# One transfer for the maxima of four heads, and the fills of the spare rows moved to the projections, in a decoder layer

## The chip, the cores and the metric

The kernel runs on one core of a Trainium2 chip. The metric is the device time of one execution in microseconds (us). The kernel before has a median of 663.38 us over three runs (662.83 to 667.53).

## The reference

A pre-norm decoder layer on x of shape (4, 1024, 256), in float32. What matters here are the two attentions, with 16 heads of 16 features each:

```python
# S: windowed causal attention, windows of W = 128 rows, each row sees its window and the one before
scores = jnp.einsum('bhcqd,bhckd->bhcqk', qc, kcat) / HD ** 0.5
scores = jnp.where(mask[None, None], scores, -jnp.inf)
attn = jax.nn.softmax(scores, axis=-1)
out = jnp.einsum('bhcqk,bhckd->bhcqd', attn, vcat)
...
# X: attention on a context of 77 rows
scores = jnp.einsum('bhqd,bhkd->bhqk', q, k) * scale
scores = jnp.where(mask == 0, jnp.asarray(-jnp.inf, scores.dtype), scores)
attn = jax.nn.softmax(scores, axis=-1)
...
x = x + attn_S(layernorm(x)); x = x + attn_X(layernorm(x), ctx); x = x + ffn(layernorm(x))
```

The feed-forward part quantises its inputs and weights to 8 bits; it is not touched by the change.

## The kernel before, in words

Attention is done in eight jobs, one for each batch and kind, in the order S0, S1, S2, X0, S3, X1, X2, X3. A job has two groups g of eight heads. q and k lie transposed, features on partitions: a group's tile has four slots of SL = 32 partitions, and a slot holds two heads of 16 features. Of each tile there are two copies, o = 0 and o = 1. In the products for head o, one operand has the other head's 16 rows masked to zero, so that a matmul over 32 rows gives the scores of one head. The rows of the other head are therefore spare, and one of them, row (1 - o) * 16 of each slot, carries the maxima: q holds the negated maximum of each query row there, k holds ones, and so the second product comes out with the maximum already taken off.

The steps of a group (g, o), by function:

- `project` (L346): 16 matmuls (L306) into ps_p, then on ScalarE two passes: L377 copies ps_p into one copy of q or k, L378 makes the masked other copy. For X jobs (q alone) L364 and L367 do this, and two transfers (L371) fill spare rows of the odd copy with zeros and ones.
- `maxima` (L724): the scores with queries on partitions, 16 records of L735 for each unit of two row tiles (S) or 32 of L750 (X), read by VectorE (L765 with the causal mask, L776) into mx. An S group has four units, an X group two.
- `put_maxima` (L784): a transpose of mx (L787), a copy to mxT of 32 x 128 on ScalarE (L791), for S jobs a transfer that fills the ones row of k (L793), and four transfers (L801), one for each slot, that write mxT's rows into the spare row of q.
- `weights` (L816): the scores with keys on partitions (L827 for S, L856 for X), which read the put rows, then the exponential on ScalarE (L837, L859) and for S the causal mask on POOL (L841).
- `weighted_values` (L862): L871 and L881, then VectorE transposes (L895) and normalises.

The order is written out by a small planner at the end of `attention`: a list of units, and in slot s the weights of unit s and the maxima of unit s + 5 (LEAD). Projections, values, output projections and preparations of weights are put into slots by due times and costs; within a slot come weighted values, these tasks, then `put_maxima`, `maxima`, `weights`. Each engine gets its instructions in that order and runs them in it. `put_maxima` of a group stands one slot before its first weights for S jobs, three for X jobs.

All these transfers go out on SP's queue (queue_of[0]), in the order written: rows of maxima, fills, and the loads of weights still to come (the context weights L471, the context L491, the feed-forward weights L629 and L656). An instruction on SP waits for its inputs and holds up those behind it. The first halves of the first job are projected before a branch on the mask (L1555); the branch taken here is the one with equal mask rows.

Of the kernel before, what the change touches and what calls it, by code (L numbers as in the profile page):

```python
# [13 lines left out]
AF = mybir.ActivationFunctionType  # L14
# [4 lines left out]
P = 128  # L19
# [6 lines left out]
def decoder_layer(  # L26
# [32 lines left out]
    nc = tc.nc  # L59
    B, S, D = x.shape  # L60
    SK = ctx_in.shape[1]
    FF = w_gate.shape[0]
    NT = S // P
    NC = D // P
    H, HD, SL = 16, 16, 32
    NP = 2
    NS = 2
    NJ = 4
    NH = 2
    HT = NT // NH  # L70
# [131 lines left out]
    with ExitStack() as att:  # L202
# [7 lines left out]
        def bank(name):  # L210
            return ps_b.tile([P, 512], F32, name=name, tag="b")
# [5 lines left out]
        rows, onerow, nextrow = [], [], []  # L217
        for o in range(NS):
# [3 lines left out]
            for dst, first, n in (  # L222
# [7 lines left out]
                    out=at[:, :, 0:n],  # L230
                    in_=at[:, :, 0:n],
                    compare_op=ALU.not_equal,
                    fill=1.0,
# [10 lines left out]
        none_one = []  # L244
        for row in range(2):
            t = wp.tile([NJ, P], F32, name=f"fill{row}")
# [5 lines left out]
            out=f,  # L252
            in_=f,
            compare_op=ALU.is_ge,
            fill=NEG,
# [20 lines left out]
        def next_of(key, tiles):  # L276
            turn[key] += 1
            return tiles[(turn[key] - 1) % len(tiles)]
# [24 lines left out]
        def by_columns(out, lhsT, rhs, **on):  # L303
            for k in range(NJ):
                r = slice(k * SL, (k + 1) * SL)
                nc.tensor.matmul(out[r], lhsT[:, r], rhs, skip_group_check=True, **on)  # L306
# [24 lines left out]
        def normed_T(job, hf):  # L331
# [11 lines left out]
                    nc.scalar.copy(xnT[:, c, :], ps)  # L343
            job.xnT[hf] = xnT

        def project(job, g, which, hf):  # L346

            out = job.q if which == "q" else job.k
            w = job.wq if job.kind == "X" else (wq_s if which == "q" else wk_s)
            if hf == 0:  # L350
                for o in range(NS):
                    out[g, o] = next_of("qk", qks)
            ps = bank("ps_p")
            for c in range(NC):
                by_columns(
                    ps,
                    w[:, c, g * P : (g + 1) * P],
                    job.xnT[hf][:, c, :],
                    start=(c == 0),
                    stop=(c == NC - 1),  # L360
                )
            half = [out[g, o][:, hf * HS : (hf + 1) * HS] for o in range(NS)]
            if job.kind == "X":
                nc.scalar.activation(  # L364
                    half[1], ps, AF.Identity, bias=job.bq[:, g : g + 1], scale=QSCALE
                )
                nc.scalar.activation(  # L367
                    half[0], half[1], AF.Identity, bias=nextrow[0], scale=rows[0]
                )
                for row in range(2):  # L370
                    queue_of[0].dma_start(  # L371
                        out=half[1][row : P : SL, :].rearrange("j (t q) -> j t q", q=P),
                        in_=none_one[row].unsqueeze(1).to_broadcast([NJ, HT, P]),
                    )
                return
            first = 1 if which == "q" else 0
            nc.scalar.activation(half[first], ps, AF.Copy, scale=QSCALE if which == "q" else 1.0)  # L377
            nc.scalar.activation(half[1 - first], half[first], AF.Copy, scale=rows[1 - first])  # L378


        leading = Job("S", 0)
        for hf in range(NH):
            st = stats_of(leading, hf)
            st.tiles(0, HT, True)
            st.end()
            normed(leading, hf, range(HT))
            if hf == 0:
                masked = wgT.rearrange("p c f -> p (c f)")[:, : NT * SK]
                nc.vector.tensor_scalar(masked, m_all, 0.0, None, ALU.is_equal)
                ones_bf = wuT[:, 0, 0:P]  # L390
                nc.gpsimd.memset(ones_bf, 1.0)
                normed_T(leading, 0)
                for which in ("q", "k"):
                    project(leading, 0, which, 0)
                ps_n = bank("ps_n")
                for t in range(NT):
                    nc.tensor.matmul(
                        ps_n[:, :SK],
                        ones_bf,
                        masked[:, t * SK : (t + 1) * SK],  # L400
                        start=(t == 0),
                        stop=(t == NT - 1),
                    )
# [12 lines left out]

        begun = dict(turn)
        begin.close()
        queue_of = [nc.sync]

        def attention(alike):
            turn.update(begun)
            queue_of[0] = nc.sync if alike else nc.scalar
# [6 lines left out]
            for i in range(5):  # L430
                t = wp.tile([P, 2, H + 1, HD + 1], F32, name=f"vt{i}")
# [352 lines left out]
            def put_maxima(job, g, o):  # L784

                ps = bank("ps_mx")
                nc.tensor.transpose(  # L787
                    ps[: NJ * NT, :P], job.mx[g, o].rearrange("p j t -> p (j t)"), ident
                )
                mxT = work.tile([NJ * NT, P], F32, name="mxT", tag="mxT", bufs=2)  # L790
                nc.scalar.copy(mxT, ps[: NJ * NT, :P])  # L791
                if job.kind == "S":
                    queue_of[0].dma_start(  # L793
                        out=job.k[g, o][(1 - o) * HD : P : SL, :].rearrange(
                            "j (t q) -> j t q", q=P
                        ),
                        in_=none_one[1].unsqueeze(1).to_broadcast([NJ, NT, P]),
                    )
                for j in range(NJ):
                    row = j * SL + (1 - o) * HD  # L800
                    queue_of[0].dma_start(  # L801
                        out=job.q[g, o][row : row + 1, :],
                        in_=mxT[j * NT : (j + 1) * NT, :],
                    )

            def weight_bias(job, g, o, u):

# [304 lines left out]
            first, last = -LEAD, N + 8  # L1112
# [23 lines left out]
            def project_all(job, g, hf, *when):  # L1136
                for which, (a, by) in zip(("q", "k") if job.kind == "S" else ("q",), when):
                    task(a, by, 1.0, project, job, g, which, hf)

            for j, job in enumerate(jobs):  # L1140
# [4 lines left out]
                for hf in range(NH):  # L1145
# [41 lines left out]
                    g = NP - 1  # L1187
# [43 lines left out]
            for slot in range(first, last):  # L1231
# [6 lines left out]
                if slot == N:  # L1238
# [7 lines left out]
                    while beside:  # L1246
                        t = min(beside, key=lambda t: t[1:3])
# [13 lines left out]
                while t := next_in(tasks, slot, spent, cap):  # L1261
# [3 lines left out]
                    if fn is out_project:  # L1265
                        job, hf, t2 = args
# [9 lines left out]
                for args in puts.get(slot, ()):  # L1276
                    put_maxima(*args)
# [332 lines left out]
```

## Time and profile before

| | |
|---|---|
| median of three runs | 663.38 us (662.83 to 667.53) |
| profiled execution, its own time | 661.71 us |
| its span | 660.0 us |
| mean granted TensorE clock | 0.986 |
| transfers of maxima (L801), 4 KB each | 128 |
| fills of X kind (L371), 8 KB each | 32 |
| ones fills (L793), 16 KB each | 16 |
| attention, S and X jobs | about 18 to 540 us |

How to read the lines: "PE" is TensorE's matmuls, "PEld" its weight loads, "DVE" VectorE, "ACT" ScalarE, "POOL" GpSimd, "SPq" the queue on which transfers are issued. A line of the timeline gives start, length, engine, source line, operation, output and inputs, number of instructions merged, and in brackets how long the engine had been idle before and what ended that. A line of the view of one tile gives the number of instructions with their shortest, median and longest duration in ns, or an engine that waited for the tile with the time in us and how often. A line of the view by stretches gives busy us of each engine with the number of instructions in brackets, then the granted TensorE clock as a share of full speed, the busy share of the DMA engines and the GB/s moved.

### The profile page before, as it was taken

To read this page: it belongs to the slowest core of one execution; us is meant where nothing else is said; L and a number is where in the kernel's file an instruction comes from. 1 tells how busy PE (TensorE), PEld (TensorE's weight loads), DVE (VectorE), ACT (ScalarE), POOL (GpSimd) and SP (SyncE) were. 2 spreads that over 40 slices of the span, in tenths; PEclk is the share of its full clock that TensorE was granted. 3 is DMA by queue.
4 is the path that set the end of the run, shared out by engine and by line. 5 is a ranking of instruction groups with operands and counts; after the bars stand their busy time and mean duration, and the time that the engine had idled before them with its cause. 6 is when DMAs were issued, how large, how long until landed. Compare 5 with 4: busy or idle time off the path is not lost.

```text
span 660.0 us, 20192 instructions
## 1 busy us (share of the span) xinstructions
PE 607.4 (92%) x7862; PEld 347.5 (53%) x7862; DVE 541.5 (82%) x1915; ACT 366.8 (56%) x672; POOL 268.6 (41%) x522
## 2 busy tenths in 40 slices
PE   9899999999999989989999999999999997878774
PEld 6456556566565655544456655544434345334564
DVE  5778878788689798578997986888878787799896
ACT  2365655644656536455565365447466565698392
POOL 3164633645227487440064866526601141111032
PEclk9999999999999999799999999999999999899898
DMA  8100100000000000000000000000000110000057
GB/s 289 51 5 16 38 4 20 4 5 23 3 28 12 11 12 14 5 22 18 5 11 11 13 26 28 5 4 6 4 4 6 35 65 17 1 0 1 1 96 164
DMA packets 19293, 17.93 MB, mean 27 GB/s; under 512 B 3190, under 2 KB 18551, under 8 KB 19191
## 3 DMA queue, kind: packets, MB, share of 16 engines
q1 hardware_dynamic: 16999, 14.74, 7.0%
q0 software_dynamic: 1904, 1.84, 2.1%
q8 instruction: 64, 1.05, 0.6%
q14 instruction: 38, 0.31, 0.1%
q10 hardware_dynamic: 288, 0.00, 0.0%
HBM read 9.47 MB, written 6.03 MB: 23 GB/s over the span
## 4 chain that ended last, share of the span: by engine, by line
PE 56%; DVE 30%; ACT 6%; issue 6%; POOL 1%; DMA 1%; DVEq 0%; ACTq 0%
PE ps_p L306 11%; PE ps_av L871 7%; PE sc_n L735 7%; PE sc_t L827 6%; PE ps_op L306 6%; DVE junk L765 5%; PE ps_av L881 3%; DVE o_sb L895 3%; PE ps_v L306 3%; DVE bnst L192 2%; PE sc_n L750 2%; PE sc_t L856 2%; DVE aT L917 2%; PE ps_idle L117 2%; DVE x L935 2%
## 5 line engine op out<-in xcount | busy, mean ns | idle before, releaser
L765 DVE CUSTOM_DVE_ANT_0 junk<-sc_n,cboth 128x256 bf16<-128x256 f32 (+1 forms) x512 | 172.7, 403 | 33.1 <-PE sc_n L735 32.7
L837 ACT ACTIVATE pt<-sc_t 128x512 f32<-128x512 f32 (+1 forms) x256 | 125.4, 577 | 84.3 <-PE sc_t L827 83.1
L841 POOL TENSOR_SCALAR_AFFINE_SELECT pt<-pt 128x256 f32<-128x256 f32 x256 | 101.7, 407 | 113.1 <-ACT pt L837 102.9
L859 ACT ACTIVATE ptx<-sc_t 77x512 f32<-77x512 f32 x128 | 65.2, 596 | 36.1 <-PE sc_t L856 36.1
L827 PE MATMUL sc_t<-shared 32*128 32x256 f32 (+1 forms) x1024 | 79.8, 371 | 2.9 <-DMA shared<-mxT 1.8
L735 PE MATMUL sc_n<-shared 32*128 32x256 f32 (+1 forms) x1024 | 75.1, 387 | 2.7 <-ACT shared L377 1.2
L322 POOL TENSOR_SCALAR xn<-x,mv,rs 128x256 f32<-128x256 f32 x56 | 69.7, 1251 | 0.0
L827 PEld LDWEIGHTS sc_t<-shared 32*128 32x128 f32 x1024 | 61.6, 186 | 11.0 <-ACT mxT L791 2.7
L160 POOL TENSOR_SCALAR ve<-mv 128x4 f32<-128x4 f32 x20 | 4.6, 232 | 153.3 <-DVE mv L194 153.3
L895 DVE STREAM_TRANSPOSE o_sb<-ps_av 128x512 f32<-128x512 f32 x63 | 45.0, 714 | 24.4 <-PE ps_av L871 15.3
L306 PE MATMUL ps_p<-shared,w_s 128*32 128x512 f32 x512 | 60.9, 595 | 3.3 <-DVE mx L776 1.7
L735 PEld LDWEIGHTS sc_n<-shared 32*128 32x128 f32 x1024 | 46.1, 184 | 33.3 <-DVE mx L765 12.6
L871 PE MATMUL ps_av<-pt,vt 128*32 128x256 f32 (+1 forms) x1152 | 60.3, 353 | 3.0 <-DVE mx L765 2.6
L776 DVE TENSOR_REDUCE mx<-sc_n 128x4 f32<-128x308 f32 x128 | 51.8, 467 | 8.7 <-PE sc_n L750 8.5
L871 PEld LDWEIGHTS ps_av<-pt,vt 128*32 128x32 f32 x1152 | 35.5, 112 | 31.9 <-issue 6.9
L765 DVE DVE_READ_ACCUMULATOR2_ANT mx<- 128x1 f32 x512 | 42.9, 84 | 0.0
L856 PE MATMUL sc_t<-shared,kx 32*77 32x512 f32 x256 | 42.8, 598 | 0.0
L377 ACT ACTIVATE shared<-ps_p 128x512 f32<-128x512 f32 x32 | 19.1, 597 | 38.7 <-PE ps_p L306 38.7
L881 PE MATMUL ps_av<-ptx,vx 77*32 77x512 f32 x256 | 36.0, 605 | 4.8 <-DVE mx L776 3.1
L750 PEld LDWEIGHTS sc_n<-kx,shared 32*128 32x128 f32 x1024 | 31.7, 186 | 10.2 <-DVE mv L194 1.7
L750 PE MATMUL sc_n<-kx,shared 32*128 32x77 f32 x1024 | 36.4, 277 | 0.0
L1423 ACT ACTIVATE act<-pg,gsc 128x512 f32<-128x512 f32 x44 | 29.2, 687 | 11.6 <-PE pg L1408 8.9
(200 smaller groups left out, 990.7 us busy)
## 6 DMA issues: line engine op xcount, KB each, us to landing
x<-in_x_dram SPq DMA_DIRECT2D x8, 512.0 KB
out_dram<-shared SPq DMA_DIRECT2D x9, 256.0 KB
shared<-mxT SPq DMA_DIRECT2D x128, 4.0 KB
out_dram<-x SPq DMA_DIRECT2D x7, 256.0 KB
out_dram<-shared POOLq DMA_DIRECT2D x7, 256.0 KB, 4.5
w_s<-in_L_attn_w_qkv_dram SPq DMA_DIRECT2D x2, 384.0 KB
raw_d<-in_L_ffn_w_down_dram SPq DMA_DIRECT2D x2, 352.0 KB
raw_f<-in_L_ffn_w_gate_dram SPq DMA_DIRECT2D x5, 128.0 KB
```

What stands on the lines that cost most here:

```text
L306: nc.tensor.matmul(out[r], lhsT[:, r], rhs, skip_group_check=True, **on)
L322: eng.tensor_scalar(xn, xb[job.b][:, t, :], job.st[hf].mv[:, i, 0:1], job.st[hf].rs[:, i : i + 1], ALU.subtract, ALU.mult,)
L735: nc.tensor.matmul(banks[j][:, (i + 1) * 2 * P - n : (i + 1) * 2 * P], q[r, t * P : (t + 1) * P], k[r, k0 * P : k0 * P + n], start=True, s ...
L750: nc.tensor.matmul(banks[j][:, i * SK : (i + 1) * SK], q[r, t * P : (t + 1) * P], k[r, :], start=alike, stop=alike or i == HT - 1,)
L765: nc.vector.tensor_tensor_reduce(out=junk[:, 2 * P - n :], in0=banks[j][:, (i + 1) * 2 * P - n : (i + 1) * 2 * P], in1=cboth[:, 2 * P - n ...
L827: nc.tensor.matmul(banks[j][:, w : w + n], k[r, t * P : (t + 1) * P], q[r, t * P : t * P + n], start=True, stop=True,)
L837: nc.scalar.activation(pt.rearrange("p i a q -> p (i a q)")[:, :w], banks[j][:, :w], AF.Exp)
L841: nc.gpsimd.affine_select(out=pt[:, :, 0, :], in_=pt[:, :, 0, :], compare_op=ALU.is_ge, fill=0.0, base=0, pattern=[[0, 2], [1, P]], channe ...
L856: nc.tensor.matmul(banks[j][:SK], k[r, :], q[r, s], start=alike, stop=True)
L859: nc.scalar.activation(pt, banks[j][:SK], AF.Exp)
L871: nc.tensor.matmul(ps[j * SL : (j + 1) * SL, (a0 - t0) * P : (a1 - t0) * P], slot_of(job.vs[kb // 2][:, kb % 2], heads[j]), job.pts[g, o, ...
L895: nc.vector.transpose(job.av[g, o, hf], ps)
```

## The change

The four row transfers of `put_maxima` become one transfer with the 32 rows of mxT as its source and the spare row of all four slots as its target. The ones fill of k leaves `put_maxima`. In its place `project` fills spare rows beside every S projection: for q, the max row of the odd copy is set to zero over the half that was projected; for k, the ones row of the even copy is filled by a transfer, and the odd copy gets its ones from the bias of the second ScalarE pass (`onerow`, a 1 at that row), which was a plain scaled copy. The fills read `none_one`, two small tiles of zeros and ones; `queue_of` is made before the first projections. For X jobs the same two fills are issued as before, through the helper.

```diff
+        queue_of = [nc.sync]
+
+        def fill(half, row, value):
+            queue_of[0].dma_start(
+                out=half[row : P : SL, :].rearrange("j (t q) -> j t q", q=P),
+                in_=none_one[value].unsqueeze(1).to_broadcast([NJ, HT, P]),
+            )
+
         def project(job, g, which, hf):
...
-                for row in range(2):
-                    queue_of[0].dma_start(
-                        out=half[1][row : P : SL, :].rearrange("j (t q) -> j t q", q=P),
-                        in_=none_one[row].unsqueeze(1).to_broadcast([NJ, HT, P]),
-                    )
+                fill(half[1], 0, 0)
+                fill(half[1], 1, 1)
                 return
             first = 1 if which == "q" else 0
             nc.scalar.activation(half[first], ps, AF.Copy, scale=QSCALE if which == "q" else 1.0)
-            nc.scalar.activation(half[1 - first], half[first], AF.Copy, scale=rows[1 - first])
+            if which == "q":
+                nc.scalar.activation(half[0], half[1], AF.Copy, scale=rows[0])
+                fill(half[1], 0, 0)
+            else:
+                nc.scalar.activation(
+                    half[1], half[0], AF.Identity, bias=onerow[1], scale=rows[1]
+                )
+                fill(half[0], HD, 1)
...
                 nc.scalar.copy(mxT, ps[: NJ * NT, :P])
-                if job.kind == "S":
-                    queue_of[0].dma_start(
-                        out=job.k[g, o][(1 - o) * HD : P : SL, :].rearrange(
-                            "j (t q) -> j t q", q=P
-                        ),
-                        in_=none_one[1].unsqueeze(1).to_broadcast([NJ, NT, P]),
-                    )
-                for j in range(NJ):
-                    row = j * SL + (1 - o) * HD
-                    queue_of[0].dma_start(
-                        out=job.q[g, o][row : row + 1, :],
-                        in_=mxT[j * NT : (j + 1) * NT, :],
-                    )
+                queue_of[0].dma_start(
+                    out=job.q[g, o][(1 - o) * HD : P : SL, :].rearrange(
+                        "j (t q) -> j t q", q=P
+                    ),
+                    in_=mxT,
+                )
```

`half` is the projected half of the tile's columns (HT = 4 tiles of 128), NJ is 4 slots, NT is 8 tiles.

More of the change, by code (lines that the diff above doesn't have):

```diff
@@ L418, in decoder_layer @@
         begin.close()
-        queue_of = [nc.sync]
         def attention(alike):
```

## The prediction

> **What bounds the kernel now.** I read the page first: busy times, then the slices and the granted clock.
>
> ```profile
> span 660.0 us, 20192 instructions
> PE 607.4 (92%) x7862; PEld 347.5 (53%) x7862; DVE 541.5 (82%) x1915; ACT 366.8 (56%) x672; POOL 268.6 (41%) x522
> ...
> PEclk9999999999999999799999999999999999899898
> ```
>
> TensorE is busy 92% of the span and VectorE 82%; the two pass scores and maxima to each other in a fixed order, so time is lost only where TensorE stands still and VectorE has no backlog to live on. The one 7 in the clock row (slice 17, about 264 to 280 us) is such a place. Next I asked who waits for the transfers that the change merges: the view of tile mxT.
>
> ```profile
> L801 SPq DMA_DIRECT2D shared<-mxT x128: 621/635/857, 32.2 to 525.0; - x128
> ...
> who waited for it (us, times):
>   PEld sc_t L827: 2.7, 6
>   PEld sc_t L856: 2.3, 4
>   PE sc_t L827: 2.1, 4
> ```
>
> One issue holds the SP queue 0.635 us, so the four of a group go out over 2.7 us; yet all waits for them come to a few us in 32 groups. The trace records every increment of a transfer's semaphore. By the last one, a row of maxima (L801) lands 1.78 us after its issue begins, a fill of the X kind (L371, 4 x 4 pieces of 512 B) 1.88, and a ones fill (L793, 4 x 8 pieces) 2.33. I set the last landing of each group against its first weight matmul (L827 or L856). All 16 X groups have 3.4 to 15 us to spare; of the S groups two are late by 0.96 and 1.80 us, both last of their batch, before an X job (265.46 and 396.01 us); four are late by 0.6 or less. The worst:
>
> ```profile
> 261.38 0.39 SPq L629 DMA_DIRECT2D raw_f<-in_L_ffn_w_gate_dram  x1
> ...
> 261.87 0.56 SPq L793 DMA_DIRECT2D shared<-fill  x1
> ...
> 262.52 2.75 SPq L801 DMA_DIRECT2D shared<-mxT  x4
> ...
> 265.46 3.14 PE L827 MATMUL sc_t<-shared 32*128 32x256 f32 x16 [1.30 <-DMA shared<-mxT]
> ...
> 268.52 3.64 PE L871 MATMUL ps_av<-pt,vt 128*32 128x128 f32 x40
> ```
>
> mxT was written at 260.27, but the queue held two X fills, a weight load and the ones fill first. The clock by stretches shows what the stall cost further:
>
> ```profile
> core 0: us, PE busy (x) PEld busy (x) DVE busy (x) ACT busy (x) POOL busy (x), PEclk, DMA share, GB/s
> ...
> 263.20:266.50 3.30, 2.00 (x38) 1.50 (x38) 1.63 (x4) 1.46 (x2) 0.76 (x2) 1.00 0.04 12
> 266.60:269.90 3.30, 3.30 (x30) 2.01 (x34) 0.00 (x0) 2.03 (x4) 1.20 (x3) 0.50 0.02 5
> 270.00:273.30 3.30, 3.30 (x34) 2.00 (x24) 1.00 (x3) 0.00 (x0) 1.10 (x2) 0.50 0.02 5
> ```
>
> After the gap TensorE ran 6.8 us at half clock, with VectorE idle for 6.43 us.
>
> **The change, part by part.** Counts on SP in the S and X jobs: 128 row transfers become 32, 16 ones fills go, 32 new fills come (one per q or k projection of an S job): 80 issues fewer. The merged put has the ones fill's outer shape (4 x 8 pieces), so I price its landing like L793, 2.33 us, with 1.78 (a row) as the low end. Before, the last row landed 2.06 + 1.78 = 3.84 us after the first issue; it is 1.5 us earlier now, and the weights wait once, not four times.
>
> Gains. (1) The group at 265.46: without the ones fill the put goes out at about 261.7 and lands at 264.05; TensorE is free at 264.1. Sc_t takes 1.04 us (its length in groups that do not wait), the ps_av after it 1.94 (the same work at 398.98), ps_t 1.06 (at 16.86): ps_mx, at 273.63 before, can start at about 268.2. Gain 5.4; if the clock drops all the same, 2. The xn tiles are there early (POOL ends them at 260.8), so nothing else is late next. (2) The group at 396.01: it ended at 399.05; the put now leaves at 393.1, right behind the 352 KB raw_d load, which landed at 395.62 (the ones fill behind it at 395.70), so 395.9 + 1.04 = 396.9: gain 2.1, between 1.0 and 2.5. (3) The four small ones are 0.77, 0.41, 0.26 and 0.33 longer than 1.04; after the first TensorE waits for VectorE anyway (37.23 us). I take 0.5 of 1.77. Sum: 8.0.
>
> Losses: the new waits. A maxima matmul (L735) now waits for a fill after the projection's second ScalarE pass, on q for odd heads and on k for even ones. q fills have at least 15 us to their reader. k fills need about 2.0 us (0.09 because the pass with bias is 0.813 as in L367 and not 0.722 as in L378, 0.03 to issue, 1.88); 13 of 16 have 4.1 us or more. Three have none:
>
> ```profile
> 16.86 1.06 PE L337 MATMUL ps_t<-ident,xn 128*128 128x128 f32 x8
> 18.64 1.80 PE L735 MATMUL sc_n<-shared 32*128 32x128 f32 x32 [0.72 <-ACT shared L343]
> 20.39 3.64 PE L306 MATMUL ps_p<-shared,w_s 128*32 128x512 f32 x32
> 24.77 2.01 PE L735 MATMUL sc_n<-shared 32*128 32x256 f32 x32 [0.74 <-ACT shared L377]
> ```
>
> (4) The first maxima, 18.64: the k pass ends at 18.04 (L378), so by the row the fill lands at 20.03; but the last two x loads, ahead on the same queue, land at 19.44 and 20.69, and a small transfer behind a big one landed 0.08 after it (395.70). I take 20.7: +2.1, between 1.4 and 2.7. (5) Maxima of tile 4, 24.77: pass ends 25.47, landing 27.47: +2.7. (6) The same in batch 3, TensorE at 315.28: pass ends 315.98, landing 317.98; VectorE had other work until 316.71 and would get its scores 1.16 later (as 25.93 after 24.77), at 319.1: +2.4. What queues behind these waits is all of TensorE's stream, and VectorE with it.
>
> SP order: fills that wait for ScalarE now stand ahead of weight loads. With the ScalarE ends of the trace, craw leaves 9.1 us later (lands 84.5, read at 90.5: free), Wv 8.0 later (landing 123.7 against a read at 122.59: (7) +1.1), Wq 9.8 later (173.7 against 173.39: (8) +0.3), one raw_f 11.8 later (213.2 against 214.4: free, barely); other moved loads keep 2 us or more. Puts of S groups behind a fill lose at most 0.5 of their 1.5. VectorE's and POOL's streams are unchanged; ScalarE's 16 longer passes (+1.5 us) lie beside matmuls, at 56% busy. Sum of (4) to (8): 8.6.
>
> The clock. The new gaps, with the idle already there, are 2.8 (17.9 to 20.7), 3.4 (to 27.5) and 3.2 us (to 318). The row above shows a drop after a 3.3 us stretch with 2.00 busy, part of which was waiting inside; stretches with 1.83, 1.79 and 1.70 busy of 3.3 (549.9, 283.7, 553.3 us) were followed by full clock, ones with 1.51 and 1.22 (563.6, 618.2) by 3.41 us at 0.50. So drops are likely; a window at half clock costs 1.7 us where TensorE sets the pace. Ends: nothing, and two windows (3.4) at each, 10.2. I take 1.2, 0.4 (VectorE has 16 x 0.345 = 5.5 us of scores to read there) and 1.2: 2.8, nearer the low end because one window is the commoner row.
> [...]
>
> Sum on the profiled execution (661.7 us for a span of 660.0): 661.7 - 8.0 + 8.6 + 2.8 = 665.1. The median of the runs, 663.38, lies 1.7 above that execution; carried over, 666.8.
>
> **The rivals.** R1, clock stays up at the new gaps: the last term is 0 and the time 664.0. For it: the longest gaps may split over two windows. R2, slower: each of the three new gaps drops the clock for two windows, as after 265.46, where the row shows 6.8 us. Then the term is 10.2 and the time 674.2. It decides (over 1%) from a clock term of 6.0 up, two double drops. Against it: the one-window rows, and VectorE's backlog after 27.5. R3, the put was hidden anyway: the stalls at 265 and 396 are due to the loads ahead on the queue, and the merged put lands no earlier. Gains fall to about 0.5 and the time rises to 674.3. Against it: the ones fill at 261.87 landed at 264.10, in the very place that the put takes. R4, a little faster: no drops, (4) at its low end, TensorE later by (4) and (5) at its read of Wv and Wq than these loads are, so that (7) and (8) go, and (2) and (3) at their high ends: 664.0 - 0.7 - 1.4 - 0.4 - 1.3 = 660.2. Against it: the loads are late by the same ScalarE passes that shift too.
>
> **How the numbers follow.** Forecast 0.50, R1 0.24, R2 0.10, R3 0.06, R4 0.10. A measurement of this kernel can tell about 1%, 6.6 us, from no change. Range: 660.2 (R4) up to 672.0 (forecast with two of the three drops doubled, +3.4, and the ends of (2) and (4), +1.1 and +0.6), leaving out most of R2 and R3. Slower than 670.0: R2, R3 and a few of the forecast's own, 0.16. Faster than 656.7 needs gains without most losses, 0.03. Within: 0.81.
>
> **What would show it.** In the new profile: TensorE's first L735 group about 2 us later and the third 5 us later, each with an idle time of 2.5 to 3.5 before it, ended by a fill; the same in batch 3, first head group; no wait for mxT longer than 0.3 and no half clock after the last S group of batch 2; ps_w of Wv waiting 1 us. If TensorE starts its first maxima at 18.6, (4) is wrong and with it the queue reading; if the merged put lands 3 us or more after its issue, (1) and (2) are.

## The result and the profile after

| | before | after |
|---|---|---|
| median of 12 runs, us | 662.89 (662.3 to 667.53) | 665.93 (663.3 to 669.18) |
| span of the profiled execution, us | 660.0 | 663.4 |

The changed kernel takes 1.0039 times as long (95% interval 1.0021 to 1.0058): 3.0 us more, where 3.4 were forecast (666.8 against the 663.38 known then). The two profiled executions differ by 3.4 us, so they can be laid side by side.

The page of the changed kernel, the three lines that were shown of before:

```profile
span 663.4 us, 19988 instructions
PE 604.7 (91%) x7857; PEld 345.1 (52%) x7862; DVE 542.1 (82%) x1915; ACT 368.6 (56%) x672; POOL 268.3 (40%) x522
...
PEclk9899999999999999989899999999999999899899
```

The engines do the same work. In the clock row the 7 at 264 to 280 us is gone, and three 8s are new: slice 2 (17 to 33 us), slice 18 (282 to 299) and slice 20 (315 to 332).

The view of tile mxT, and three lines of the view of waits (us in total, times, longest), both of the changed kernel:

```profile
L802 SPq DMA_DIRECT2D shared<-mxT x32: 528/542/599, 36.7 to 526.0; - x32
...
who waited for it (us, times):
...
  PE sc_t L830: 0.8, 3
```

```profile
PE sc_n L745 <- DMA shared<-fill: 9.2, 3, 3.6
...
PE ps_w L490 <- DMA raw_w<-in_L_xattn_Wv_dram: 1.3, 1, 1.3
...
PE ps_w L490 <- DMA raw_w<-in_L_xattn_Wq_dram: 0.4, 1, 0.4
```

One issue of 0.54 us stands in place of four of 0.64, and TensorE's waits for the maxima fell from 2.1 to 0.8 us (those of its weight loads, 2.7 and 2.3, are as before). In their place it waits 9.2 us for fills, in three places, and 1.7 us for two weight loads; before, the view has neither.

To see where the time went I set the start of each unit's scores and weights in one trace against the same unit in the other (L735 has become L745, L827 L830, L871 L874, and L306 is the same). Up to the end of attention the two traces run in parallel between these steps, to 0.3 us:

| place, us in the trace of after | shift, us | step of the prediction |
|---|---|---|
| 19.56, first maxima | +0.92 | (4) |
| 28.50, maxima of tile 4 | +2.81, then +0.47 at half clock | (5) |
| 39.74, 186.83, 226.21 and 358.35, weights of the four small late groups | -0.56, -0.35, -0.20 and -0.27 | (3) |
| 127, read of Wv | +1.39 | (7) |
| 181, after the read of Wq | +0.53 | (8) |
| 269.02, last S group of batch 2 | -1.48 and -4.36, then +0.58 | (1) |
| 285.00, next projection | +1.63 at half clock | none |
| 319.63, batch 3, first head group | +2.84, then +0.87 at half clock, -0.33 | (6) |
| 406, after the last S group of batch 3 | -1.89 | (2) |

Losses 8.49, half clock 2.97, gains 7.73 at the two late groups and 1.38 at the four small ones, +0.58 and -0.33 behind (1) and (6): the sum is +2.60. At the end of attention the shift is +3.22; the 0.6 between are in shifts below 0.3 us each. The feed-forward part, which the change leaves alone, adds 1.0 more, with one half-clock window that the trace of before does not have (561.39), and the tail behind the last matmul gives 0.8 back: +3.4 in all.

The first of the four small groups, before and then after:

```profile
35.50 1.81 PE L827 MATMUL sc_t<-shared 32*128 32x256 f32 x16
```

```profile
39.74 1.04 PE L830 MATMUL sc_t<-shared 32*128 32x256 f32 x16
```

The timeline of TensorE in the changed kernel, at the first two losses:

```profile
15.99 1.24 PE L337 MATMUL ps_t<-ident,xn 128*128 128x128 f32 x8
19.56 1.80 PE L745 MATMUL sc_n<-shared 32*128 32x128 f32 x32 [2.34 <-DMA shared<-fill]
21.31 3.64 PE L306 MATMUL ps_p<-shared,w_s 128*32 128x512 f32 x32
28.50 3.45 PE L745 MATMUL sc_n<-shared 32*128 32x256 f32 x32 [3.55 <-DMA shared<-fill]
```

Both score groups now wait for a fill, 2.34 and 3.55 us, where before they waited 0.72 and 0.74 us for ScalarE. The second also runs 3.45 us in place of 2.01: the clock. The same view further on, at the gain, at the place that nobody had named, and at the third loss:

```profile
268.07 1.13 PE L760 MATMUL sc_n<-kx,shared 32*128 32x77 f32 x32
269.02 1.09 PE L830 MATMUL sc_t<-shared 32*128 32x256 f32 x16
270.04 1.94 PE L874 MATMUL ps_av<-pt,vt 128*32 128x128 f32 x40
...
281.50 1.13 PE L760 MATMUL sc_n<-kx,shared 32*128 32x77 f32 x32
282.45 0.88 PE L830 MATMUL sc_t<-shared 32*128 32x256 f32 x16
285.00 3.55 PE L306 MATMUL ps_p<-shared,w_s 128*32 128x512 f32 x16 [1.67 <-DVE mx L786]
...
319.63 2.09 PE L745 MATMUL sc_n<-shared 32*128 32x256 f32 x16 [3.34 <-DMA shared<-fill]
```

The weights at 269.02 take 1.09 us where they took 3.14, with no wait in front, and the weighted values behind them 1.94 where they took 3.64. At 285.00 the projection waits 1.67 us for VectorE; before, it waited just as long (285.21), but now it then runs at half clock. The view by stretches shows the new half-clock windows (columns as in the prediction):

```profile
25.50:28.90 3.40, 0.40 (x8) 0.43 (x12) 0.27 (x2) 0.95 (x2) 0.00 (x0) 1.00 0.02 5
28.90:32.30 3.40, 3.40 (x36) 2.53 (x32) 2.12 (x13) 0.00 (x0) 0.00 (x0) 0.50 0.02 5
281.50:284.90 3.40, 1.83 (x49) 1.61 (x48) 3.26 (x8) 1.95 (x6) 3.32 (x5) 1.00 0.17 43
284.90:288.30 3.40, 3.30 (x16) 0.59 (x16) 1.84 (x7) 0.14 (x1) 3.40 (x6) 0.50 0.00 0
315.60:319.00 3.40, 0.69 (x10) 0.11 (x2) 2.54 (x8) 1.41 (x2) 0.00 (x0) 1.00 0.01 2
319.10:322.40 3.30, 2.77 (x24) 1.89 (x24) 0.69 (x3) 0.00 (x0) 0.00 (x0) 0.50 0.15 40
```

Each is one window. Ahead of two of them TensorE was nearly idle (0.40 and 0.69 busy of 3.40); ahead of the one at 284.9 it was busy 1.83 of 3.40, just over half.

### The profile page after: what moved, and what is told of

Read it like the earlier page. It is cut to its first block, busy times and chain, and to the rows that moved or that the text cites. A ratio compares the mean times of both kernels' runs of the same rounds, so it can differ in the third digit from the quotient of the medians.

```text
span 663.4 us, 19988 instructions
## 1 busy us (share of the span) xinstructions
PE 604.7 (91%) x7857; PEld 345.1 (52%) x7862; DVE 542.1 (82%) x1915; ACT 368.6 (56%) x672; POOL 268.3 (40%) x522
## 4 chain that ended last, share of the span: by engine, by line
PE 55%; DVE 29%; ACT 6%; issue 6%; DMA 2%; POOL 1%; SPq 0%; DVEq 0%; ACTq 0%
PE ps_p L306 11%; PE ps_av L874 7%; PE sc_n L745 7%; PE ps_op L306 6%; PE sc_t L830 5%; DVE junk L775 5%; PE ps_av L884 4%; DVE bnst L192 3%; PE ps_v L306 3%; DVE o_sb L898 3%; PE sc_t L859 2%; PE sc_n L760 2%; DVE aT L920 2%; PE pg L1411 2%; DVE aN L908 2%
## 5 line engine op out<-in xcount | busy, mean ns | idle before, releaser
L745 PE MATMUL sc_n<-shared 32*128 32x256 f32 (+1 forms) x1024 | 77.5, 398 | 10.0 <-DMA shared<-fill 9.2
L830 PE MATMUL sc_t<-shared 32*128 32x256 f32 (+1 forms) x1024 | 74.7, 367 | 1.5 <-DMA shared<-mxT 0.5
L745 PEld LDWEIGHTS sc_n<-shared 32*128 32x128 f32 x1024 | 48.1, 189 | 40.4 <-issue 15.9
L306 PE MATMUL ps_p<-shared,w_s 128*32 128x512 f32 x512 | 62.5, 609 | 3.4 <-DVE mx L786 1.7
L830 PEld LDWEIGHTS sc_t<-shared 32*128 32x128 f32 x1024 | 58.7, 185 | 7.7 <-ACT mxT L801 2.7
L874 PE MATMUL ps_av<-pt,vt 128*32 128x256 f32 (+1 forms) x1152 | 58.6, 346 | 3.0 <-DVE mx L775 2.6
L874 PEld LDWEIGHTS ps_av<-pt,vt 128*32 128x32 f32 x1152 | 34.6, 109 | 31.1 <-DVE mx L775 6.8
L760 PEld LDWEIGHTS sc_n<-kx,shared 32*128 32x128 f32 x1024 | 31.7, 186 | 10.9 <-issue 3.1
L760 PE MATMUL sc_n<-kx,shared 32*128 32x77 f32 x1024 | 36.5, 277 | 0.0
```

What stands on the lines that cost most here:

```text
L745: nc.tensor.matmul(banks[j][:, (i + 1) * 2 * P - n : (i + 1) * 2 * P], q[r, t * P : (t + 1) * P], k[r, k0 * P : k0 * P + n], start=True, s ...
L760: nc.tensor.matmul(banks[j][:, i * SK : (i + 1) * SK], q[r, t * P : (t + 1) * P], k[r, :], start=alike, stop=alike or i == HT - 1,)
L830: nc.tensor.matmul(banks[j][:, w : w + n], k[r, t * P : (t + 1) * P], q[r, t * P : t * P + n], start=True, stop=True,)
L874: nc.tensor.matmul(ps[j * SL : (j + 1) * SL, (a0 - t0) * P : (a1 - t0) * P], slot_of(job.vs[kb // 2][:, kb % 2], heads[j]), job.pts[g, o, ...
```

## The experiments

Theory A is the prediction's account: the merged put gains at two late groups, and the fills lose it again at a few places, three score groups that wait for a k fill and two weight loads behind fills. Rival B: the put gained little (hidden anyway, R3). Rival C: the fills cost a little everywhere, through the queue or the longer ScalarE passes. All ratios are to the kernel before, with 95% intervals.

**Each half alone.** First, the merged put without the moved fills, as an edit of the kernel before:

```diff
-                for j in range(NJ):
-                    row = j * SL + (1 - o) * HD
-                    queue_of[0].dma_start(
-                        out=job.q[g, o][row : row + 1, :],
-                        in_=mxT[j * NT : (j + 1) * NT, :],
-                    )
+                queue_of[0].dma_start(
+                    out=job.q[g, o][(1 - o) * HD : P : SL, :].rearrange(
+                        "j (t q) -> j t q", q=P
+                    ),
+                    in_=mxT,
+                )
```

> The kernel before with the merged put alone; the ones fill stays ahead of it, no new fills. Theory (the two halves of the change pull in opposite ways): the late group at the end of batch 2 gets its put at 262.5 + 1.87 = 264.4 instead of up to 266.4, so its weights start about 264.4 and the half clock after it goes; 5 to 6 us there, 1.9 to 2.2 at the end of batch 3 (396), nothing elsewhere: 655 to 657. Rival (the transfer was hidden, the gain in the changed kernel came from the ones fill leaving the queue): within 1.5 us of 662.9.

Measured: 657.89 us, ratio 0.9927 (0.9906 to 0.9948). The two late groups give 4.30 and 1.89 us in its trace. B falls: the put was not hidden. The forecast of this run was about 1 us too good. Two things hold it back. The ones fill still stands ahead of the put (at the end of batch 2 the fill was issued at 261.50 and the put at 262.15), and TensorE still waits 1.9 us for the maxima, as the view of mxT in this run shows:

```profile
L799 SPq DMA_DIRECT2D shared<-mxT x32: 523/538/666, 31.4 to 518.0; - x32
...
  PE sc_t L827: 1.9, 4
```

And the clock dropped at two places where before had none, 280.78 (+1.58) and 62.33 (+1.31). The second is odd, as the view by stretches of this run shows:

```profile
58.90:62.30 3.40, 2.99 (x22) 1.57 (x16) 3.40 (x19) 2.06 (x4) 2.36 (x6) 1.00 0.00 0
62.30:65.70 3.40, 3.40 (x28) 2.59 (x26) 3.07 (x20) 0.12 (x1) 1.15 (x6) 0.50 0.02 5
```

TensorE was busy 2.99 of the 3.40 us ahead of that drop (0.88), and its longest idle time there was 0.41 us.

Then the moved fills with the four row transfers, as an edit of the changed kernel (as all that follow, unless said):

```diff
-                queue_of[0].dma_start(
-                    out=job.q[g, o][(1 - o) * HD : P : SL, :].rearrange(
-                        "j (t q) -> j t q", q=P
-                    ),
-                    in_=mxT,
-                )
+                for j in range(NJ):
+                    row = j * SL + (1 - o) * HD
+                    queue_of[0].dma_start(
+                        out=job.q[g, o][row : row + 1, :],
+                        in_=mxT[j * NT : (j + 1) * NT, :],
+                    )
```

> The changed kernel with four row transfers instead of the merged one: only the fills are moved. Theory: all the losses of the changed kernel (0.9, 2.8, 1.4, 0.5, 2.8 and about 0.8 of half clock, 9.2 in all) and of the gains only what the ones fill's 0.65 us on the queue was worth: 669 to 673. Rival (the moved fills cost little, the loss comes from the merged put waiting for its last row): 663 to 666.

Measured: 676.3 us, ratio 1.0216 (1.019 to 1.0241), above the expected range. This is the median of four runs; the profiled execution is the fastest of them, 672.93. The fill waits are 9.3 us, and the losses stand at the same places with the same sizes (+2.80 at tile 4, +1.26 at Wv, +2.87 in batch 3). Of the gain at the last S group of batch 2, 3.77 of 5.84 us are there, since the ones fill is out of the way; of the 1.89 us in batch 3 only 0.55 are, and of the gains at the four small groups none, so these are mostly the merging's. Two half-clock windows that the changed kernel lacks or has smaller (+1.37 at 69.5, +1.70 at 291.4) belong to the surplus.

The halves do not add up: 4.8 us less and 13.6 us more would be 8.8 us more, and together they make 3.0. In the profiled spans it is -3.1, +11.2 and +3.4, a surplus of 4.7. The half-clock terms that I can read off are 2.89, 4.74 and 2.97 us, which is 4.66 of surplus; the gain at 269 counted in both halves goes the other way by 2.2, and what makes that good I could not divide.

**No fill for k.** Both copies of k come from PSUM on ScalarE with mask and bias; the q fills stay:

```diff
...
-                nc.scalar.activation(half[1], half[0], AF.Identity, bias=onerow[1], scale=rows[1])
-                fill(half[0], HD, 1)
+                for o in range(NS):
+                    nc.scalar.activation(half[o], ps, AF.Identity, bias=onerow[o], scale=rows[o])
```

> The changed kernel, but k's even copy gets its ones row as the odd one does, from the bias of a masked ScalarE pass, so no fill stands between a k projection and its maxima; the zero fills of q stay. Theory (the cost is three waits of TensorE for k fills and two weight loads queued behind them): the waits on a fill fall from 9.2 us to under 0.5, Wv and Wq are there in time, 665.9 - 9.2 = 656.7, between 655 and 658.5. Rival (32 fills cost by their traffic and place on the queue, whichever they are): half of them are left, so half the loss: 661 to 662.

Measured: 658.93 us, ratio 0.9946 (0.9927 to 0.9965), 0.4 us above the range. No wait for a fill is left, and with them 7 us of the changed kernel's time are gone (665.93 to 658.93). The edit brings a cost of its own at six places, about 0.7 us each. Here is one, first ScalarE and then TensorE in this run, then TensorE before the change:

```profile
94.50 1.45 ACT L387 ACTIVATE shared<-ps_p,onerow,rows 128x512 f32<-128x512 f32 x2 [1.07 <-PE ps_p L306]
```

```profile
95.32 1.80 PE L829 MATMUL sc_t<-shared 32*128 32x256 f32 x16
```

```profile
94.02 1.04 PE L827 MATMUL sc_t<-shared 32*128 32x256 f32 x16
```

The projection's PSUM bank is read by both passes, until 95.95, and not by the first alone: 0.85 us longer. The weights that take this bank next are 0.76 us longer than before.

**No fill in any S job.** On top of the last edit, the same for q, with masks times the scale of q (`rowsq`):

```diff
...
-                nc.scalar.activation(half[1], ps, AF.Copy, scale=QSCALE)
-                nc.scalar.activation(half[0], half[1], AF.Copy, scale=rows[0])
-                fill(half[1], 0, 0)
+                for o in range(NS):
+                    nc.scalar.activation(half[o], ps, AF.Copy, scale=rowsq[o])
```

> As the kernel with k by bias, and q's odd copy masked on ScalarE too, so that S jobs have no fills at all; every copy of q and k is now made straight from PSUM. In the trace of k by bias, six groups of weights after a k projection took about 0.7 us more than the same groups before (sc_t 1.80 and not 1.04 at 95.3 us), where the second pass holds the projection's PSUM bank 0.85 us longer. Theory A (the held bank costs, the fills of q don't): q's second pass holds it as well, 2 to 4 us more than k by bias, 661 to 663. Theory B (the fills of q cost by their place on the queue): faster than k by bias, 656 to 658.

Measured: 664.02 us, ratio 1.0008 (0.9992 to 1.0023), 1 us above the range that was expected if the held bank costs. With no fill at all in the S jobs the kernel is 5 us slower than with the q fills. So the q fills cost less than the means of doing without them, which shows at 12 places at least with 0.34 to 0.75 us each. This speaks against C, though it does not price the q fills themselves.

**The clock at the waits.** To keep TensorE busy through the waits at the first maxima of tile 4 in batch 0 and in batch 3, 28 matmuls with zeros were put ahead of them, into the PSUM bank that the scores then overwrite:

```diff
                 if job.kind == "S":
                     k = job.k[g, o]
+                    if (job.b, g, o, u) in ((0, 0, 0, 2), (3, 0, 0, 2)):
+                        idle(banks[0], 28)
```

> The changed kernel with 28 matmuls on zeros (L117's kind) ahead of the maxima that wait for a fill, in batch 0 and in batch 3, so that TensorE works while it waits. Their results are overwritten. Theory (the gap itself costs 2.8 us each time, the half clock after it 0.3 to 0.9 more): no stretch at 0.50 after 28.9 and 319, 664.5 to 665.5. Rival (half clock is what the waits cost): 662 to 664. If the zeros' matmuls take longer than the wait, 666 to 667.

Measured: 664.19 us, ratio 1.0022 (1.0007 to 1.0037), which overlaps the changed kernel's interval, so no gain in time is shown; it lies between the two expected ranges. The clock stays up after both waits, and the +0.87 in batch 3 is gone. But a half-clock window now lies at 20.42, after the first maxima's wait, which had none in the changed kernel, and set against the first maxima, those of tile 4 start 4.41 us later than before (2.81 in the changed kernel). So which gap gets the drop is not fixed by its length. What differs is its place in the steps of 3.413 us, counted from the changes of clock in each trace: the gap ahead of the first maxima, 2.27 us here, lies within one step, 17.01 to 20.42 (1.13 busy of 3.40, then half clock), while that of the changed kernel, 2.34 us, is cut in two by a border at 18.67 (1.96 and 2.52 busy of 3.41 on its two sides, full clock after both).

**The k fill of the even copy back in its old place**, ahead of the put of even groups; everything else as changed:

```diff
-                fill(half[0], HD, 1)
...
                 nc.scalar.copy(mxT, ps[: NJ * NT, :P])
+                if job.kind == "S" and o == 0:
+                    queue_of[0].dma_start(
+                        out=job.k[g, o][HD : P : SL, :].rearrange("j (t q) -> j t q", q=P),
+                        in_=none_one[1].unsqueeze(1).to_broadcast([NJ, NT, P]),
+                    )
```

> The changed kernel, but the ones of k's even copy are filled where they were before, ahead of the put of an even group; the odd copy keeps its bias and q its zero fill, and no ScalarE pass is changed. Theory: no maxima wait for a fill, Wv and Wq are there in time, and both late groups (odd ones) have their merged put without a ones fill ahead: 656 to 658, like the put alone (657.9) or 0.5 less. Rival (the zero fills and the 0.09 us longer pass have a price): 659 or more.

Measured: 653.87 us, ratio 0.9865 (0.9837 to 0.9892), 2 us better than the range and faster than both kernels. TensorE at the first two losses in this run:

```profile
21.40 1.80 PE L744 MATMUL sc_n<-shared 32*128 32x128 f32 x32 [0.71 <-ACT shared L343]
23.15 3.64 PE L306 MATMUL ps_p<-shared,w_s 128*32 128x512 f32 x32
27.53 2.01 PE L744 MATMUL sc_n<-shared 32*128 32x256 f32 x32 [0.74 <-ACT shared L382]
```

The waits are those of before again, 0.7 us for ScalarE. (This execution began its first maxima 2.8 us later than that of before, ahead of anything the edit touches.) All gains are kept, to the hundredth: -1.48, -4.36 and -1.89. Both weight loads are in time. From 17.5 to 553 us the clock never dropped.

**Only the three late fills away.** The changed kernel with the bias in place of the fill for the three k projections whose readers wait, and no others:

```diff
+            if which == "k" and (job.b, g, hf) in ((0, 0, 0), (0, 0, 1), (3, 0, 1)):
+                for o in range(NS):
+                    nc.scalar.activation(half[o], ps, AF.Identity, bias=onerow[o], scale=rows[o])
+                return
```

> The changed kernel with the k projections ahead of the three waiting maxima (batch 0, first head group, both halves; batch 3, first head group, second half) masked by ScalarE with a bias, the other 13 k fills and all q fills kept. Theory (the loss is at three places and at two loads): 0.9 + 2.8 + 2.8 + 0.9 us go, 1.4 + 0.5 for Wv and Wq stay, up to 1 for banks held longer: 658 to 660. Rival (each fill costs a little): 3 of 32 fills go, 665.

Measured: 655.79 us, ratio 0.9891 (0.9867 to 0.9916), 2 us better than the range. Without three of the 16 k fills 10 us of the changed kernel's time are gone (in the changed kernel's trace 1.63 of them are the half-clock window at 285; this one has another instead, at 62.40); the other 29 S fills, 16 for q and 13 for k, stay in this kernel, and it is 7 us faster than before. C falls with this.

**And the two loads earlier.** On top of that edit, the loads of Wv and Wq (pieces 4 and 7 of the context weights) written one slot sooner:

```diff
-                    task(at + k, at + k, 0.3, fn)
+                    early_load = k == 0 and i in (4, 7)
+                    task(at + k - early_load, at + k - early_load, 0.3 * (not early_load), fn)
```

> As the kernel with three k projections by bias, and the loads of Wv and Wq written one slot earlier, ahead of the k fill that held them on SP's queue; TensorE's order is the same. Theory: TensorE's wait of about 1.4 us for Wv and 0.5 for Wq goes, 1.5 to 2 us less than without it, 656.5 to 658. Rival (these waits have cover, what follows waits for VectorE anyway): the same time within 0.5 us.

Measured: 654.42 us, ratio 0.9873 (0.9846 to 0.9901), again 2 us better than the range. The shifts at Wv (+1.87 in the run without this edit) and Wq (+0.42) are gone from its trace, which is A's reading of (7) and (8). The gain in the medians, 1.4 us, is smaller than the intervals, so as a time it is not separated. Between this version and the one before the last (653.87) there is no difference either.

## Why the prediction held

The time lay 0.9 us from the forecast, and most terms hold one by one. Three sizes, of the put's landing, (3) and (4), and the reading of the clock do not. By the shifts the terms come to 2.6 us and not to 3.4; shifts that no term names fill the 0.8 between, so that part of the agreement is luck.

- **Gains.** (1) was priced at 5.4; it gave 5.84, less 0.58 once VectorE set the pace again. (2) gave 1.89 of 2.1. (3) was mis-sized: 0.5 was taken of 1.77, and the four groups gave 1.38, in the same four sizes with the put alone. Only behind the first did TensorE stand still again, for 0.13 us. The landing was mis-sized as well: the put lands 1.87 us after its issue, not 2.33, so the outer shape that it shares with the ones fill did not set its price. (1) does not rest on that: in its sum the put was there at 264.05 and TensorE free at 264.1, and the trace shows no wait ahead of 269.02.
- **(4), first maxima.** The queue was read from the wrong part of the big load. The k fill was issued at 17.32 and landed at 19.43, 2.11 us later, while the last x load, issued ahead of it on the same queue, landed at 20.66. Its semaphore tells more: 15 of the 16 increments of that load came by 19.31, and only the last at 20.66, so the fill landed 0.12 us behind the fifteenth. The trace of before has the same straggler (19.41, then 20.69). The pair from which I took the rule has none: the increments of raw_d came from 395.20 to 395.62, and the ones fill landed at 395.70. So the small transfer came in behind nearly all of the big one both times, but it did not wait for the last part (19.43 against 20.66). For (2) the rule held: the put landed at 400.98, 0.21 us behind raw_d (400.77), and the weights there still waited 0.5 us for it. The wait in (4) grew by 1.62 us, near the low end given (1.4), not by 2.1; as a shift it is +0.92, since the matmuls ahead of it ended 0.7 earlier in this execution.
- **(5) and (6).** +2.81 for 2.7 and +2.84 for 2.4; the pass, the issue and the landing add up as they were summed. The relief by VectorE's other work in (6) came later, as -0.33, and not at the wait; 0.25 of it was lost again at 332.7.
- **(7) and (8).** +1.39 for 1.1 and +0.53 for 0.3. Behind the fills the load of Wv went out at 124.67 and that of Wq at 175.87, where before it was 112.87 and 160.96; less the shifts ahead of them (3.6 and 5.0) that is about 8 and 10 us later, as forecast. In the run without the earlier loads TensorE waits 1.8 and 0.3 us for the two; in the run with them it reads Wv at 121.28 with no wait ahead.
- **The clock.** 2.97 us in the trace for 2.8 priced, but only in sum. I had 1.2 for the first gap, 0.4 for the second, 1.2 for batch 3. They were none, 0.47 and 0.87. The largest, 1.63 at 285, was in no list: TensorE waits there for VectorE as long as before, 1.67 us, and before it went on at full clock. Its window was as little busy then (0.54) as now (0.54), though with other work in it, as shown below. That the clock term came out right is luck; without that window the time would have been near R1's 664.0.
- **The rivals.** R3 falls by the put alone. R2 needed double drops; every new drop is a single window. R4 needed no drops and both loads in time; the trace has three new drops in attention and waits of 1.3 and 0.4 us for the loads.

What stays open is what decides a drop. The length of a gap and the busy share do not settle it: a window 0.88 busy at about 60 to 66 us was followed by a drop in four of the kernels and by none in four others, the version with 653.87 among them. With the put alone it was 2.99 busy of 3.40 from 58.90 and the clock then 0.50; in the changed kernel it was 3.00 of 3.41 from 63.05 and the clock then 1.00. What the traces do show is a grid: in each of the ten, all changes of the clock lie a whole number of steps of 3.4133 us apart, to 0.002 us (in the changed kernel's 1, 75, 76, 85 and 86 of them after 28.91), and against the work these steps lie elsewhere in each trace.

So each trace can be cut into windows along its own grid, and then one sees what ran in them. At 285 the window of before held the projection behind the wait, as its stretch and its timeline show:

```profile
283.70:287.00 3.30, 1.79 (x16) 0.42 (x16) 3.20 (x10) 1.55 (x4) 3.30 (x7) 1.00 0.15 40
```

```profile
285.21 1.92 PE L306 MATMUL ps_p<-shared,w_s 128*32 128x512 f32 x16 [1.67 <-DVE mx L776]
```

That of the changed kernel, 281.50 to 284.91, held score products alone (L760 and L830 above) and then the wait. This is a pattern in all ten traces. In attention (17 to 540 us), of 1520 windows at full clock, 14 were followed by a drop (in the kernel before 1 of 151, in the changed kernel 3 of 149). In 13 of these, all work but score products filled less than 0.2 of the window; in the last it filled 0.21, with TensorE idle for 0.67. Of the 1433 windows in which other work filled more than 0.22, none was followed by a drop, though TensorE stood idle for up to 0.49 of one. Windows with 0.03 or less of other work were always followed by a drop when at most 0.61 busy, and not in the two cases of 0.98 and more. Why score products should differ from other matmuls here was not shown. The pattern was found after the runs, and no run tests it.

## What to carry to other kernels

A transfer that is moved forward to be out of one consumer's way must be checked against its new first reader: 13 of 16 k fills landed 2.1 to 10.8 us ahead of their first reader, and the three that had no such room took back all that the merging gained. When a change pairs a gain and a loss, time each half alone and then repair only the instances that are late; here that turned +3.0 us into -9.0. A second pass that reads PSUM rather than the finished copy was not free where the bank is taken again at once (about 0.7 us at each of six places).

## What the runs showed of the hardware

- In the changed kernel transfers of one queue overlap, and one overtook another: the 8 KB fill of k, issued at 17.32, landed 1.23 us ahead of a 512 KB load issued at 11.55, but 0.12 us behind the fifteenth of that load's 16 increments. With that load in flight the q fill issued at 15.53 took 3.72 us to land; the median of the 64 fills of this shape is 1.87. The semaphore of the k fill climbs in five steps, at 18.28, 0.96 us after its issue began, and then four times from 19.00 to 19.43; that of the load climbs in 16, from 18.29 to 20.66.
- A put from 32 source rows into the spare row of four slots landed in 1.87 us (median of 32 in the changed kernel), 0.46 faster than a fill of such a row in four slots from broadcast source rows (2.33, median of 16 in the kernel before).
- Half clock came after a window in which TensorE was 0.88 busy with no idle time over 0.41 us, at about 60 to 66 us in four kernels of eight (with the put alone 2.99 of 3.40 from 58.90, then 0.50). Such a window held score products alone.
- All changes of the clock in each of the ten traces lie on one grid of 3.4133 us (in the changed kernel 1, 75, 76, 85 and 86 steps after 28.91).
- Holding a projection's PSUM bank for 0.85 us more cost about 0.7 us at each of the six places where the next weights took it, in the run without a fill for k (at 95.32 it was 0.76).
